# Query norms of half a sequence from four column tiles, inverse roots once per half, in a two-layer transformer kernel on one core

## The chip, the cores and the metric

The kernel runs on one core of one Trainium2 chip, as one launch. The metric is the device time of that launch in microseconds, taken as the median of several runs. Everything is float32, and [...] the profile shows two records (a weight load and a matmul each) for one matmul of the code; a transpose is one record.

The engines are named as in the profile: PE is TensorE's matmuls and PEld its weight loads, DVE is VectorE, ACT is ScalarE, POOL is GpSimd, SP is the engine whose queue issues most of the DMAs. Each engine works through its own queue of instructions in order and waits there for what it needs of the others.

## What is computed

The reference is a model of two layers over 16 sequences of 256 tokens, 128 wide. Each layer is an attention part and a feed-forward part with residuals and layernorms. The change lies in the last of these parts, a causal attention with 16 heads of 64, whose queries and keys are divided by their norm before the scores are made, with a mixture of experts behind it:

```python
def l2norm(x, eps=1e-12):
    return x / jnp.sqrt(jnp.sum(x * x, axis=-1, keepdims=True) + eps)
h = layernorm(x, ln_g, ln_b)
q = (h @ Wq).reshape(B, S, H, DH).transpose(0, 2, 1, 3)
k = (h @ Wk).reshape(B, S, H, DH).transpose(0, 2, 1, 3)
v = (h @ Wv).reshape(B, S, H, DH).transpose(0, 2, 1, 3)
q = l2norm(q) * q_scale
k = l2norm(k) * k_scale
logits = jnp.einsum('bhid,bhjd->bhij', q, k) * QK_SCALE
...
attn = jax.nn.softmax(logits, axis=-1)
out = jnp.einsum('bhij,bhjd->bhid', attn, v)
```

So each token has, for each of 16 heads, a sum of 64 squares of its query and one of its key, and the inverse root of each.

## The kernel before

The 4096 tokens are cut into 8 groups of 512 (two sequences). Each group passes through five stages: A, a dense attention with 16 heads; B, a routed feed-forward; C, a linear and a windowed attention with a gate; D, the causal attention with normed queries and keys; E, the eight experts. Several groups are under way at a time in different stages.

The order of the work is not written by hand. Each piece of work is handed to a planner, `W.add(engine, cost in ns, function, r=reads, w=writes)`, and `Plan.order` (lines 143 to 234) makes a list out of it: again and again it takes the piece that can begin first by its own costs (ties go to the lower `at`, a due time in units of groups), on whichever engine may do it ("VS" means DVE or ACT). The engines then get their instructions in that order. A buffer (`W.buf`) belongs to a class with a fixed number of slots (`SLOTS`, lines 39 to 62: six tiles for `x`, two for `xT`, six for `ud` and so on); a piece can only begin when its buffers have slots, so the number of slots sets how far stages run ahead of each other. `hold` reserves the slot for a later piece. A matmul's `mode` ("f" full, "r" row tiles, "c64" and "c32" column tiles) tells the planner when TensorE changes its tiling. An object such as `chain_d` that several pieces write keeps them in the order in which they were added. The `x` tiles of the first six groups are loaded at the start, those of the last two by the SP queue when a slot is free (`load_x`, line 287).

Stage D (`stage_d`, line 1153) makes a layernorm of the group, transposes it to `hT` (line 1160), and then handles each sequence in two halves of two units; a unit is four heads. There are 64 units in all, 32 halves. `unit` (line 1163) does this:

- the keys of 256 tokens, tokens on partitions (line 1177); ACT squares them into `sq_k` (1178), a copy is kept in `kn` (1179), DVE sums the squares of each head into columns 8 to 15 of `nqk` (1182);
- the queries, already transposed, head by head along the partitions (1191); ACT squares them into `sq_q` (1192), and `keep` (1194) writes them times a scale to `qT`;
- the norms of the queries (1204 to 1207): the squares lie along the partitions, so TensorE adds them up. For each 128 tokens and pair of heads, the 128x128 squares are the stationary operand, and `blk2` (line 487), two columns of ones, one for each head, is the moving one; eight columns come out, tokens on partitions, and DVE copies them to `nqk` (1210);
- `rsqrt` (lines 1135 to 1151): the inverse roots of 16 columns by a bit trick and three Newton steps on DVE, twelve small operations;
- the values (1212), the keys times their inverse roots on POOL (1217), the keys transposed by TensorE (1227) and copied to `kT` (1232);
- two pairs of heads (`pair`, line 568): scores (590), causal mask and maximum on DVE (597, 602, 604), the exponential on ACT with the query's inverse root as scale (623), reciprocal of the sums (630), the weights times it on POOL (636), four or three transposes of the weights (651), and the product with the values (675).

`into_width` (678) then projects the four results of a half.

All matmuls go through `mm` (line 514), where the first argument is the output, then the stationary and the moving operand. The lines of the norms:

```python
for t in range(2):
    for i in range(2):
        mm(pq()[:, 4 * t + 2 * i : 4 * t + 2 * i + 2], sq_q()[:, i * S + t * P : i * S + (t + 1) * P], blk2)
```

Stage C has a place where TensorE works in four column tiles (line 1078): products with `vm` and with `hones` go to 32 output partitions each, four of them side by side.

Of the kernel before, what the change touches and what calls it, by code (L numbers as in the profile page):

```python
# [12 lines left out]
ALU = mybir.AluOpType  # L13
# [17 lines left out]
NFC = FF // P  # L31
NEG = -1.0e30
EPS = 1e-5
NX = 6
NBURST = 2

OFF = {"a": 0.0, "b": 1.0, "c": 2.0, "d": 3.0, "e": 4.0}

SLOTS = (
    ("x", 512, 6),  # L40
    ("xT", 512, 2),
    ("ua", 512, 6),
    ("ud", 512, 6),
    ("pb", 512, 4),
    ("pt", 512, 4),
    ("ov", 256, 8),
    ("m", 64, 26),
    ("k1", 256, 5),
    ("b", 512, 2),
    ("sc", 288, 1),  # L50
    ("c", 512, 9),
    ("qm", 512, 2),
    ("pbC", 512, 2),
    ("ptC", 512, 2),
# [183 lines left out]
def kernel(ctx: ExitStack, tc: tile.TileContext, a: dict, out: bass.AP):  # L238
# [8 lines left out]
    def ctile(name, shape, dtype=F32):  # L247
        return const.tile(shape, dtype, name=name, tag=name)
# [235 lines left out]
        vms.append(ctile(f"vm{i}", [P, 4, D]))  # L484
        nc.gpsimd.memset(vms[i], 0.0)

    blk2 = ctile("blk2", [P, 2])
    nc.gpsimd.memset(blk2, 0.0)
    nc.gpsimd.memset(blk2[:DH, 0:1], 1.0)
    nc.gpsimd.memset(blk2[DH:, 1:2], 1.0)  # L490
    cmask = ctile("cmask", [P, P])
    make_causal_mask(nc, cmask, NEG)
    ones1 = ctile("ones1", [P, 1])
# [2 lines left out]


    chain_a, chain_c, chain_d = ([object() for _ in range(3)] for _ in range(3))
    end_b, end_c = object(), object()

    def pe(n, cols=P, count=1, passes=2):
        return count * passes * max(0.84 * n, 0.87 * cols)
# [62 lines left out]
        else:  # L565
            W.add("V", dve(512), lambda: nc.vector.tensor_scalar(o(), tp(), scale, shift, ALU.mult, ALU.add), r=[tp], w=[o])

    def pair(pi, qT, kT, v, ov, causal, rq):

# [20 lines left out]
        def top():  # L592
            s = sps(S2, a=2)
            n = nmx(n=4, pattern="p (a b) -> p a b", a=2)
            if causal:
                diag = s[:, :, P : 3 * P].rearrange("p a (b k) -> p a b k", k=P)
                nc.vector.tensor_tensor(  # L597
                    out=diag, in0=diag, in1=cmask.unsqueeze(1).unsqueeze(1).to_broadcast([P, 2, 2, P]), op=ALU.add
                )
                for qc in range(2):  # L600
                    c0, nk = col[qc]
                    nc.vector.tensor_reduce(n[:, :, qc], s[:, :, c0 : c0 + nk], AX.X, ALU.max, negate=True)  # L602
                rqp = rq("p (b h) -> p h b", n=8, b=2)[:, 2 * pi : 2 * pi + 2, :]
                nc.vector.tensor_tensor(out=n, in0=n, in1=rqp, op=ALU.mult)  # L604
            else:
                nc.vector.tensor_reduce(n, s.rearrange("p a (b k) -> p a b k", k=S), AX.X, ALU.max, negate=True)  # L606
# [5 lines left out]
        for par in range(2):  # L612
# [3 lines left out]
            def weigh(par=par, pb=pb):  # L616
                s = sps(S2, a=2)
                for qc in range(2):
                    c0, nk = col[qc]
                    kw = {}  # L620
                    if causal:
                        kw["scale"] = rq()[:, qc * 4 + 2 * pi + par : qc * 4 + 2 * pi + par + 1]
                    act(  # L623
                        pb()[:, c0 : c0 + nk], s[:, par, c0 : c0 + nk], AF.Exp,
                        bias=nmx()[:, 2 * par + qc : 2 * par + qc + 1],
                        accum_out=sums()[:, 2 * par + qc : 2 * par + qc + 1], **kw,
                    )
# [507 lines left out]
    def rsqrt(o, x, n, eps):  # L1135

        ve, y, u = W.buf("m", "ve"), W.buf("m", "y"), W.buf("m", "u")

        def go():
            V = nc.vector  # L1140
            V.tensor_scalar(ve(n=n), x(n=n), eps, None, ALU.add)
            yi = y(n=n).bitcast(I32)
            V.tensor_scalar(yi, ve(n=n).bitcast(I32), 1, None, ALU.logical_shift_right)
            V.tensor_scalar(yi, yi, -1.0, float(0x5F3759DF), ALU.mult, ALU.add)
            for k in range(3):
                src, dst = (y, o) if k % 2 == 0 else (o, y)
                V.tensor_mul(u(n=n), src(n=n), src(n=n))  # L1147
                V.scalar_tensor_tensor(u(n=n), u(n=n), -0.5, ve(n=n), ALU.mult, ALU.mult)
                V.scalar_tensor_tensor(dst(n=n), u(n=n), 1.5, src(n=n), ALU.add, ALU.mult)  # L1149

        W.add("V", 2465, go, r=[x], w=[ve, y, u, o])

    def stage_d(g):
        xx = xg[g]
# [5 lines left out]
        transposed(hT, xn, "D", lng2, lnb2)  # L1160
        wqf, wkf = fqk[:, 0, :], fqk[:, 1, :]

        def unit(b, p2):

            W.at = base + (4 * b + p2) / 8
            cs = slice(p2 * 256, (p2 + 1) * 256)
            qT, kT, v = W.buf("ud", "qTD"), W.buf("ud", "kTD"), W.buf("ud", "vD")
            nqk, rqk = W.buf("m", "nqk"), W.buf("m", "rqk")
            ps_q, ps_k, ps_v = W.buf("p", "psq"), W.buf("p", "psk"), W.buf("p", "psv")
            sq_q, sq_k, kn, pq, tps = W.buf("sq", "sqq"), W.buf("sq", "sqk"), W.buf("kn", "kn"), W.buf("p", "pq"), W.buf("p", "tpsk")  # L1170

            def by_tokens(ps, w):
                for t in range(2):
                    mm(ps()[:, t * 256 : (t + 1) * 256], hT()[:, b * S + t * P : b * S + (t + 1) * P], w[:, cs])


            W.add("P", pe(256, count=2), lambda: by_tokens(ps_k, wkf), r=[hT], w=[ps_k], hold=[sq_k, kn])
            W.add("S", scl(512), lambda: act(sq_k(), ps_k(), AF.Square), r=[ps_k], w=[sq_k])
            W.add("VS", (dve(512), scl(512)), lambda e: copy(e, kn(), ps_k()), r=[ps_k], w=[kn])
            W.add(  # L1180
                "V", dve(512),
                lambda: V.tensor_reduce(nqk()[:, 8:16], sq_k("p (h d) -> p h d", d=DH), AX.X, ALU.add), r=[sq_k], w=[(nqk, 1)],
            )


            def proj():
                for i in range(2):
                    p = 2 * p2 + i
                    mm(ps_q()[:, i * S : (i + 1) * S], wqf[:, p * P : (p + 1) * P], hT()[:, b * S : (b + 1) * S])

            W.add("P", pe(S, count=2), proj, r=[hT], w=[ps_q], hold=[sq_q, qT])
            W.add("S", scl(512), lambda: act(sq_q(), ps_q(), AF.Square), r=[ps_q], w=[sq_q])

            def keep(e):
                for i in range(2):
                    c, o = qks[:, 2 * p2 + i : 2 * p2 + i + 1], slice(i * S, (i + 1) * S)
                    if e == "S":
                        A.mul(qT()[:, o], ps_q()[:, o], c)
                    else:
                        V.tensor_scalar(qT()[:, o], ps_q()[:, o], c, None, ALU.mult)  # L1200

            W.add("VS", (782, 714), keep, r=[ps_q], w=[qT])

            def norms():
                for t in range(2):
                    for i in range(2):
                        mm(pq()[:, 4 * t + 2 * i : 4 * t + 2 * i + 2], sq_q()[:, i * S + t * P : i * S + (t + 1) * P], blk2)

            W.add("P", pe(2, count=4), norms, r=[sq_q], w=[pq], hold=[nqk])
            W.add("V", 70, lambda: V.tensor_copy(nqk()[:, 0:8], pq()[:, 0:8]), r=[pq], w=[(nqk, 0)])  # L1210
            rsqrt(rqk, nqk, 16, 1e-12)
            W.add("P", pe(256, count=2), lambda: by_tokens(ps_v, fv), r=[hT], w=[ps_v], hold=[v])
            W.add("SV", (scl(512), dve(512)), lambda e: copy(e, v(), ps_v()), r=[ps_v], w=[v])
            n4 = [P, 8, DH]
            W.add(
                "G", gps(512),
                lambda: G.tensor_tensor(  # L1217
                    out=kn("p (h d) -> p h d", d=DH), in0=kn("p (h d) -> p h d", d=DH),
                    in1=rqk()[:, 8:16].unsqueeze(2).to_broadcast(n4), op=ALU.mult,
                ),  # L1220
                r=[rqk], w=[kn],
            )

            def turn():
                for t in range(2):
                    for i in range(2):
                        nc.tensor.transpose(
                            tps()[:, i * S + t * P : i * S + (t + 1) * P], kn()[:, t * 256 + i * P : t * 256 + (i + 1) * P], ident
                        )

            W.add("P", pe(P, count=4, passes=1), turn, r=[kn], w=[tps], hold=[kT])
            W.add("SV", (scl(512), dve(512)), lambda e: copy(e, kT(), tps()), r=[tps], w=[kT])
            got = []
            for i in range(2):
                W.at = base + (4 * b + p2 + (i + 1) / 3) / 8
                ov = W.buf("ov", "ovD")
                pair(i, qT, kT, v, ov, True, rqk)
                got.append(ov)
            return got

        def seq(b):
            for hf in range(2):
                ovs = unit(b, 2 * hf) + unit(b, 2 * hf + 1)

                def into(ps, hf=hf):
                    o = slice(2 * b * D, (2 * b + 2) * D)
# [36 lines left out]
    def stage_e(g):  # L1283
# [10 lines left out]
        for e_ in range(NE):  # L1294
# [9 lines left out]
            pe_, hids = W.buf("p", "pe"), []  # L1304
            for c in range(NFC):
                ph, hid = W.buf("p", "phE"), W.buf("hid", "hid")
                W.add("P", pe(512), lambda ph=ph, we=we, c=c: mm(ph(), we()[:, c * P : (c + 1) * P], h2()), r=[we, h2], w=[ph], burst=burst, hold=[hid])
                ec = e_ * NFC + c
                W.add("S", 571, lambda ph=ph, hid=hid, ec=ec: act(hid(), ph(), AF.Gelu_apprx_tanh, bias=b1[:, ec : ec + 1]), r=[ph], w=[hid], table="gelut", burst=burst)  # L1309
                hids.append(hid)  # L1310
# [67 lines left out]
```

## Time and profile before

| what | us |
|---|---|
| median of 3 runs | 2264.16 (2259.54 to 2265.47) |
| the profiled execution | 2259.16 |
| its span, first to last instruction | 2257.3 |
| query norms on PE (512 records of 128x2), busy | 62.3 |
| scaling of the keys on POOL (line 1217), 64 times | 67.2 |
| sums of the keys' squares on DVE (line 1182), 64 times | 43.0 |

The granted clock of TensorE was 0.982 of full speed on the mean. In the profile's lists a group is one line of the code on one engine with one kind of operands: the output, an arrow, the inputs, then how many instructions, their busy time together and the mean of one in nanoseconds, and the idle time ahead of them with what ended it. Buffer numbers are left out of the names. In a timeline the columns are the start of a run of like instructions, how long it lasted, engine, line, operation, operands and number. The ends of matmuls are modelled and overlap the next ones; the starts tell more.

### The profile page before, as it was taken

The numbers are of one execution on the slowest core, as the hardware profiler recorded it, in microseconds if no ns is written. First come the engines' busy times: TensorE is split into PE (matmuls) and PEld (weight loads), VectorE is DVE, ScalarE is ACT, GpSimd is POOL, SyncE is SP. The second block draws the span as 40 slices with busy tenths as digits, with TensorE's granted clock in tenths as the row PEclk, the third lists the DMA queues.
The fourth block names the chain that finished last, engine by engine and source line by source line (L and its number), as shares of the span: only waits on it lengthen the run. The fifth ranks groups of instructions, "written<-read, shape, count | busy, mean of one in ns | idle before, by whom it ended". The sixth has DMA issues, their size and how long they took to land.

```text
span 2257.3 us, 50085 instructions
## 1 busy us (share of the span) xinstructions
PE 2126.6 (94%) x18474; PEld 1611.8 (71%) x18474; DVE 1711.4 (76%) x5167; ACT 1316.0 (58%) x3824; POOL 801.7 (36%) x1441
## 2 busy tenths in 40 slices
PE   6999999999999999999999999999899989989987
PEld 5777767777777677776777767777667767767755
DVE  4789898888678977688767897588876976785741
ACT  3556656666466656565565666565565645654642
POOL 6435352444143531335213352143521441330421
PEclk8999999999999999999999999999999999999998
DMA  6100000000100001100010000100011001001101
GB/s 149 24 1 2 2 1 1 2 2 20 43 16 11 2 15 38 34 1 2 15 47 20 2 1 25 48 11 2 1 38 39 7 19 37 22 7 51 29 20 42
DMA packets 61029, 47.98 MB, mean 21 GB/s; under 512 B 4609, under 2 KB 51297, under 8 KB 60785
## 3 DMA queue, kind: packets, MB, share of 16 engines
q1 hardware_dynamic: 59200, 43.09, 6.8%
q8 instruction: 146, 2.39, 0.5%
q0 software_dynamic: 1008, 0.65, 0.3%
q10 hardware_dynamic: 576, 1.05, 0.2%
q14 instruction: 99, 0.80, 0.1%
HBM read 41.89 MB, written 2.88 MB: 20 GB/s over the span
## 4 chain that ended last, share of the span: by engine, by line
PE 31%; DVE 16%; ACT 3%; issue 2%; POOL 1%; POOLq 0%; DVEq 0%; ACTq 0%
PE p L514 25%; PE p L651 2%; PE s L514 2%; DVE m L602 2%; DVE s L597 1%; ACT pb L623 1%; DVE m L606 1%; DVE m L531 1%; POOL pb L636 1%; DVE s L1053 1%; DVE m L1054 1%; PE p L1071 1%; DVE m L1147 1%; DVE pt L522 1%; DVE m L1149 1%
## 5 line engine op out<-in xcount | busy, mean ns | idle before, releaser
L636 POOL TENSOR_SCALAR pb<-pb,m 128x256 f32<-128x256 f32 (+1 forms) x1024 | 452.4, 458 | 710.6 <-DVE m L630 611.2
L1309 ACT ACTIVATE hid<-p,b 128x512 f32<-128x512 f32 x256 | 169.3, 688 | 285.3 <-PE p L514 283.8
L651 PE MATMUL p<-ident,pb 128*128 128x128 f32 x1792 | 293.8, 284 | 22.4 <-POOL pb L636 17.0
L623 ACT ACTIVATE pb<-s,m 128x256 f32<-128x256 f32 x512 | 239.0, 488 | 112.5 <-DVE m L606 100.9
L623 ACT ACTIVATE pb<-s,m,m 128x128 f32<-128x128 f32 (+1 forms) x512 | 257.7, 525 | 62.3 <-DVE m L604 47.7
L651 PEld LDWEIGHTS p<-ident,pb 128*128 128x128 f32 x1792 | 208.1, 143 | 113.6 <-POOL pb L636 66.0
L514 PE MATMUL p<-h,we 128*128 128x512 f32 x512 | 251.5, 624 | 2.9 <-ACT hid L1309 2.5
L514 PEld LDWEIGHTS p<-we,hid 128*128 128x128 f32 x2048 | 238.6, 192 | 15.6 <-issue 10.0
L514 PE MATMUL p<-we,hid 128*128 128x128 f32 x2048 | 246.9, 276 | 1.0 <-ACT hid L1309 0.7
L520 ACT COPY pt<-p 128x384 f32<-128x384 f32 (+1 forms) x316 | 168.9, 541 | 122.6 <-PE p L651 115.7
L1217 POOL TENSOR_TENSOR kn<-kn,m 128x512 f32<-128x512 f32 x64 | 67.2, 1050 | 361.9 <-DVE m L630 224.0
L606 DVE TENSOR_REDUCE m<-s 128x4 f32<-128x1024 f32 x128 | 154.7, 1214 | 32.9 <-PE s L514 32.6
L514 PEld LDWEIGHTS p<-h,we 128*128 128x128 f32 x512 | 93.3, 197 | 98.9 <-issue 63.7
L1324 DVE SCALAR_TENSOR_TENSOR e<-p,m,e 128x128 f32<-128x128 f32 x256 | 71.7, 343 | 111.8 <-PE p L514 89.7
L514 PE MATMUL s<-ua,ua 64*128 64x256 f32 x1024 | 141.9, 401 | 10.9 <-ACT pb L623 10.8
L1065 ACT ACTIVATE pbC<-s,m 128x96 f32<-128x96 f32 (+1 forms) x512 | 135.1, 382 | 16.3 <-DVE m L1054 14.1
L514 PE MATMUL s<-ud,ud 64*128 64x128 f32 (+1 forms) x1024 | 115.7, 347 | 26.1 <-ACT pb L623 25.7
L522 DVE COPY pt<-p 128x512 f32<-128x512 f32 (+1 forms) x196 | 121.1, 623 | 22.1 <-PE p L651 19.9
L514 PE MATMUL p<-pt,ua 128*64 128x256 f32 x1024 | 136.8, 389 | 0.7 <-ACT pt L520 0.7
L602 DVE TENSOR_REDUCE m<-s 128x2 f32<-128x256 f32 (+1 forms) x256 | 130.8, 552 | 4.8
L514 PE MATMUL p<-pt,ud 128*64 128x256 f32 (+1 forms) x1024 | 117.7, 341 | 4.8 <-DVE pt L522 2.6
L514 PEld LDWEIGHTS s<-ua,ua 64*128 64x128 f32 x1024 | 92.0, 189 | 41.7 <-ACT pb L623 19.9
(298 smaller groups left out, 4420.3 us busy)
## 6 DMA issues: line engine op xcount, KB each, us to landing
we<-in_L_ffn_w_dram SPq DMA_DIRECT2D x128, 256.0 KB, 2.7
x<-_attn_hidden_states_dram SPq DMA_DIRECT2D x8, 256.0 KB, 5.3
out_dram<-x SPq DMA_DIRECT2D x8, 256.0 KB, 2.2
dpad<-k SPq DMA_DIRECT2D x1, 768.0 KB, 9.4
wq<-in_L_attn_Wq_dram ACTq DMA_DIRECT2D x2, 256.0 KB
wkv<-in_L_attn_Wkv_dram ACTq DMA_DIRECT2D x2, 256.0 KB, 7.3
wkv<-in_L_attn_Wkv_dram SPq DMA_DIRECT2D x2, 256.0 KB, 7.1
wo<-in_L_attn_Wo_dram SPq DMA_DIRECT2D x1, 512.0 KB, 11.2
```

The lines of the kernel that those rows point to most:

```text
L514: nc.tensor.matmul(o, lhsT=lhsT, rhs=rhs, start=start, stop=stop)
L520: nc.scalar.copy(o, i)
L522: nc.vector.tensor_copy(o, i)
L602: nc.vector.tensor_reduce(n[:, :, qc], s[:, :, c0 : c0 + nk], AX.X, ALU.max, negate=True)
L606: nc.vector.tensor_reduce(n, s.rearrange("p a (b k) -> p a b k", k=S), AX.X, ALU.max, negate=True)
L623: act(pb()[:, c0 : c0 + nk], s[:, par, c0 : c0 + nk], AF.Exp, bias=nmx()[:, 2 * par + qc : 2 * par + qc + 1], accum_out=sums()[:, 2 * par ...
L636: eng.tensor_scalar(pb()[:, c0 : c0 + nk], pb()[:, c0 : c0 + nk], sums()[:, 2 * par + qc : 2 * par + qc + 1], 1.0, ALU.mult, ALU.mult,)
L651: nc.tensor.transpose(tps()[:, at * P : (at + 1) * P], pb()[:, c0 + kc * P : c0 + (kc + 1) * P], ident)
L1065: act(pb("p (u k) -> p u k", u=4)[:, u, :nk], s8[:, hp, :nk], AF.Exp, bias=nmx()[:, hp : hp + 1])
L1217: lambda: G.tensor_tensor(out=kn("p (h d) -> p h d", d=DH), in0=kn("p (h d) -> p h d", d=DH), in1=rqk()[:, 8:16].unsqueeze(2).to_broadcast ...
L1309: W.add("S", 571, lambda ph=ph, hid=hid, ec=ec: act(hid(), ph(), AF.Gelu_apprx_tanh, bias=b1[:, ec : ec + 1]), r=[ph], w=[hid], table="gel ...
L1324: V.scalar_tensor_tensor(m, pe_()[:, j * D : (j + 1) * D], gate()[:, j * NE + e_ : j * NE + e_ + 1], m, ALU.mult, ALU.add)
```

## The change

The query norms are made for half a sequence (two units, eight heads) at once. A new constant `hsum` has, for each of the two units, 32 columns of which two carry ones over the partitions of one head each. It is now the stationary operand, and the squares are the moving one, 128 tokens wide. For each 128 tokens and pair of heads the result goes to 32 partitions of its own, so that four such matmuls stand side by side in four column tiles, and those of the second unit are added to those of the first. The norms then lie with tokens along the free dimension; they are copied to SBUF (`nT`), transposed by TensorE, and gathered into 16 columns of `nqk`. The keys of both units follow, with 16 more columns, and one `rsqrt` of 32 columns serves the half. After it come the values, the scaling, the transposes and the pairs of both units; the projection of the values now also reads `rqk`. `pair` takes its inverse roots from the new places.

The queries of a half stay longer, so they get a class of buffers of their own (`uq`), and other classes lose slots. Up-projections of stage E get a chain, `chain_e`, that keeps them in order.

```diff
-NX = 6
+NX = 5
...
-    ("x", 512, 6),
-    ("xT", 512, 2),
+    ("x", 512, 5),
+    ("xT", 512, 1),
     ("ua", 512, 6),
-    ("ud", 512, 6),
+    ("uq", 512, 3),
+    ("ud", 512, 5),
...
-    ("k1", 256, 5),
+    ("k1", 256, 4),
...
-    ("c", 512, 9),
+    ("c", 512, 8),
...
-    blk2 = ctile("blk2", [P, 2])
...
+    hsum = ctile("hsum", [P, 2, 32])
+    nc.gpsimd.memset(hsum, 0.0)
+    for u in range(2):
+        for h in range(2):
+            nc.gpsimd.memset(hsum[h * DH : (h + 1) * DH, u, 2 * u + h : 2 * u + h + 1], 1.0)
...
-        W.add("V", 2465, go, r=[x], w=[ve, y, u, o])
+        W.add("V", 2465 + 12 * (n - 16), go, r=[x], w=[ve, y, u, o])
...
-                for t in range(2):
-                    for i in range(2):
-                        mm(pq()[:, 4 * t + 2 * i : 4 * t + 2 * i + 2], sq_q()[:, i * S + t * P : i * S + (t + 1) * P], blk2)
-
-            W.add("P", pe(2, count=4), norms, r=[sq_q], w=[pq], hold=[nqk])
-            W.add("V", 70, lambda: V.tensor_copy(nqk()[:, 0:8], pq()[:, 0:8]), r=[pq], w=[(nqk, 0)])
-            rsqrt(rqk, nqk, 16, 1e-12)
...
+                for u in range(2):
+                    for t in range(2):
+                        for i in range(2):
+                            j = 2 * t + i
+                            mm(
+                                pq()[32 * j : 32 * j + 32, :P], hsum[:, u, :], sq_qs[u]()[:, i * S + t * P : i * S + (t + 1) * P],
+                                start=u == 0, stop=u == 1,
+                            )
+
+            W.add("P", 450, norms, r=sq_qs, w=[pq], hold=[nT], mode="c32")
+            W.add("VS", (dve(P), scl(P)), lambda e: copy(e, nT()[:, :P], pq()[:, :P]), r=[pq], w=[nT])
+            W.add("P", 110, lambda: nc.tensor.transpose(pn()[:, :P], nT()[:, :P], ident), r=[nT], w=[pn], hold=[nqk])
             W.add(
-                "V", dve(512),
...
+                "V", 80,
+                lambda: V.tensor_copy(nqk("p (j m) -> p j m", n=16, m=4), pn("p (j m) -> p j m", n=P, m=32)[:, :, :4]),
+                r=[pn], w=[(nqk, 0)],
             )
...
+            rsqrt(rqk, nqk, 32, 1e-12)
+            got = []
+            for u in range(2):
+                W.at = base + (4 * b + 2 * hf + u) / 8
+                kT, v, kn = W.buf("ud", "kTD"), W.buf("ud", "vD"), kns[u]
+                ps_v, tps = W.buf("p", "psv"), W.buf("p", "tpsk")
+                W.add("P", pe(256, count=2), lambda ps_v=ps_v, u=u: by_tokens(ps_v, fv, cols[u]), r=[hT, rqk], w=[ps_v], hold=[v])
...
-                W.add("P", pe(512), lambda ph=ph, we=we, c=c: mm(ph(), we()[:, c * P : (c + 1) * P], h2()), r=[we, h2], w=[ph], burst=burst, hold=[hid])
+                W.add("P", pe(512), lambda ph=ph, we=we, c=c: mm(ph(), we()[:, c * P : (c + 1) * P], h2()), r=[we, h2], w=[ph, chain_e], burst=burst, hold=[hid])
```

## The prediction

> **What bounds the kernel now.** I read the page's head first, then busy time in stretches of 100 us, then the list of waits of TensorE alone.
>
> ```profile
> span 2257.3 us, 50085 instructions
> PE 2126.6 (94%) x18474; PEld 1611.8 (71%) x18474; DVE 1711.4 (76%) x5167; ACT 1316.0 (58%) x3824; POOL 801.7 (36%) x1441
> ...
> 0.00:100.00 100.00, 81.77 (x524) 61.25 (x524) 54.90 (x119) 42.25 (x145) 53.74 (x120) 0.93 0.43 97
> ...
> 300.00:400.00 100.00, 90.03 (x817) 70.65 (x817) 87.31 (x293) 68.27 (x203) 42.70 (x74) 0.98 0.01 2
> 400.00:500.00 100.00, 98.91 (x1065) 78.26 (x1064) 85.73 (x233) 65.91 (x224) 40.59 (x79) 0.99 0.01 2
> ...
> 2100.00:2200.00 100.00, 88.49 (x585) 63.15 (x585) 60.99 (x211) 51.35 (x150) 31.06 (x61) 0.95 0.08 22
> ...
> PE s L514 <- ACT pb L623: 37.0, 29, 5.3
> PE p L651 <- POOL pb L636: 17.0, 9, 10.2
> ```
>
> PE is busy in 94% of the span; in the stretches (columns: length, then busy us of PE, PEld, DVE, ACT, POOL) it is 88 to 99 us of each hundred once the first is over. What PE lacks, 2257.3 - 2126.6 = 131 us, is 18 us of start-up, some 28 us after 2100 where only the last group is left, and small waits, the largest kind 37 us in all. So a microsecond of work taken off PE is a microsecond of time, unless it comes back as a wait. DVE at 76% is the next engine, and 86 to 91% in some stretches. A busy PE is not an exact measure, since matmuls overlap: work is priced below by the distance from one group's start to the next.
>
> **What goes.** Per unit (64 of them) PE makes the norms with eight records of 128x2, each with a 128x128 weight load:
>
> ```profile
> 708.37 0.49 PE L651 MATMUL p<-ident,pb 128*128 128x128 f32 x3
> 708.79 0.65 PE L514 MATMUL p<-ptC,vm 96*32 96x64 f32 x32
> 709.26 0.63 PE L514 MATMUL p<-ptC,hones 96*32 96x64 f32 x32
> 709.82 0.87 PE L514 MATMUL p<-pt,ud 128*64 128x256 f32 x8
> ...
> 718.56 0.95 PE L514 MATMUL p<-blk,sq 128*128 128x2 f32 x8
> 719.37 0.53 PE L651 MATMUL p<-ident,pb 128*128 128x128 f32 x3
> ...
> 726.06 0.95 PE L514 MATMUL p<-blk,sq 128*128 128x2 f32 x8
> 726.94 1.08 PE L514 MATMUL p<-pt,ua 128*64 128x256 f32 x8
> ```
>
> 719.37 - 718.56 = 0.81 us, 726.94 - 726.06 = 0.88 us; the middle, 0.85, times 64 is **54.4 us off PE** (51.8 to 56.3).
>
> On DVE, half of the 64 root sequences go. Twelve operations of 128x16 each: the three lines of the Newton steps are 37.8 + 36.6 + 37.0 us, the three before them 12.4 + 15.0 + 14.3, 153.1 us in all; the 64 small copies of line 1210 are 64 x 0.156 = 10.0 us.
>
> **What comes, on PE.** Per half (32 of them) 16 records with 32 weight columns and 128 moving columns in four column tiles. The nearest row is the window sums above, `hones`: 32 records of 64 columns in four column tiles, the same number of columns. Its sister `vm`, followed by the same mode, takes 709.26 - 708.79 = 0.47 us; `hones`, followed by another mode, 0.56, so leaving a mode costs 0.09. Entering costs the same: three transposes take 0.42 us before `vm` where 3 x 0.11 = 0.33 is usual. A half costs 0.47 + 0.09 + 0.09 = 0.65 us, 32 halves **20.8 us**; the far end, tiles that don't overlap, is rival D. The built program agrees: 844 changes between kinds of tiling against 779, 65 more. One 128x128 transpose per half at 0.11 us (a run of transposes steps by 0.11): **3.5 us**. Work on PE: -54.4 + 20.8 + 3.5 = **-30.1 us**.
>
> [...] The row: 0.47 us for 32 records is 14.7 ns each. [...]
>
> **What comes, on DVE and ACT.** 32 root sequences of 12 operations on 128x32, priced by lines 799 and 813 of that shape (220 and 241 ns): 12 x 0.22 = 2.64 us, 84.5 us. 32 gathering copies of 128x16 at about 0.16, 5 us. 32 copies of 128x128 from PSUM, 18 on DVE and 14 on ACT in the built program, at 0.309 (copies of up to 129 columns): 5.6 and 4.3 us. DVE: -163.1 + 84.5 + 5 + 5.6 = **-68 us** of 1711. That is off the bound. It counts only through PE waits that a busy DVE causes: outside start-up and the last 57 us there are 131 - 18 - 16 = 97 us of idle PE; 4% less DVE work, 4% of them, **-4 us** (bounds: 0, and half of the 34 us that PE idles in 100:500, 700:800, 1000:1100 and 1500:1600, where DVE is over 85%, -17).
>
> **New waits.** Two, both on PE, which runs in order, so that all later matmuls queue behind them and ACT and DVE behind those.
> The transpose waits for the copy of the norms. In the built order 0.9 to 4.2 us of other PE work stand between (median 1.5, by the rows' spacings); it needs a copy of 0.31 and two hand-overs of about 0.15. Nearest row: line 855's transposes, also of a tile just made, idled 2.6 + 0.9 us (DVE, ACT) at 8 places, 0.44 each. Ends 0 and 32 x 0.44 = 14; with the work between I take 0.1 each, **+3 us**.
> The first turn of keys in a half waits for the roots, now of both units:
>
> ```profile
> 325.54 0.67 DVE L1182 TENSOR_REDUCE m<-sq 128x8 f32<-128x512 f32 x1
> ...
> 328.36 0.17 DVE L1141 TENSOR_SCALAR m<-m 128x16 f32<-128x16 f32 x1
> ...
> 330.66 0.17 DVE L1149 SCALAR_TENSOR_TENSOR m<-m,m 128x16 f32<-128x16 f32 x1
> 331.01 1.04 POOL L1217 TENSOR_TENSOR kn<-kn,m 128x512 f32<-128x512 f32 x1 [5.54 <-DVE m L1149]
> 332.11 0.42 PEld L1227 LDWEIGHTS p<-ident,kn 128*128 128x128 f32 x4
> ```
>
> The roots run 328.36 to 330.83, POOL follows after 0.18, PE 0.06 after POOL. From the last key projection: square 0.60, sum 0.67, roots 2.6, POOL 1.05, hand-overs 0.6: 5.5 us. In the built order 4.6 to 17.6 us of PE work stand there (median 8.2); two places are under 5.5, eight under 6.8. Half a microsecond at eight places: **+4 us**. Below, nothing is to be won: the old trace has 0.6 us of PE waits for `kn` on PE's own list; above stands rival C.
>
> **Edits at nothing.** The fewer slots: one `x` less delays the load of group 5 until group 0 is stored, but the built order has 106 us of PE work between group 0's last expert and that group's first transpose (101 in the old one for its group 6), against 5.3 us for a load; if that cover went, PE would stand for the tail of the norm, store and load, some 10 us at three places. One `xT`, `ud`, `c` and `k1` less change what the planner interleaves; counted in PE work, the new order ends each group's attention in stage D 7 to 41 us sooner than the old, so nothing in it has been pushed back. `chain_e` only fixes an order on PE itself: no wait. The value projections move behind the roots, where they fill PE's wait. Six fewer table loads (65 to 59) on ACT, 1.28 us each, lie beside PE. Copies of `qT` and squares are as many as before.
>
> **Sum.** -30.1 - 4 + 3 + 4 = -27 us. The profiled execution took 2259.2 us (span 2257.3 and 1.9 around it): 2232. The median of the three runs is 5 us above it, so for a median I say **2235 us**.
>
> **Rivals.** (A) The forecast, 2220 to 2250: 60%. (B) The freed DVE pays more and no wait appears: -30.1 - 17, 2212: 12%. For it, DVE near 90% in those stretches; against, PE is at 98.9 in 400:500 with DVE at 86. (C) Slower: the first turn of a half becomes the stall. If two softmax jobs of the causal pairs stand on DVE ahead of the roots (lines 597, 602 twice, 604: 0.69 + 2 x 0.55 + 0.23 = 2.0 us each), the chain is 9.5 us; summed over the 32 places what the order's distances lack of it is about 48 us: 2259 - 30 + 48 = 2277. It decides from 30 us, 0.94 per half. For it, distances were planned, not measured, and both units now hang on one root; against, those 0.6 us in the old trace, whose chain was as long. 15%. (D) The column tiles don't overlap, as if the change had no tiles: 16 x 0.107 = 1.71 us a half instead of 0.47, +40, 2272: 5%; the window sums speak against it. [...]
>
> **Numbers.** Range 2210 to 2262: it leaves out most of C, D and the lower edge of B, under 2 in 10. A change within 0.3% (7 us) can't be told from none. Faster: A, B, most of E and a little of C, 0.80; same 0.08; slower, C and D for the most part, 0.12.
>
> **What would show it.** Right: PE's busy time near 2095 us, a `sq,hsum` group stepping to its successor in 0.5 to 0.6 us, DVE near 1640, 32 root sequences at 2.5 to 2.7 us. Wrong: PE's idle time over 150 us with waits of `ident,kn` for POOL (C) or of the new transpose for a copy; [...] waits of `ident,x` for a DMA, if the `x` slot was needed.

## The result, and the profile after

The changed kernel takes 2235.34 us in the median (2233.45 to 2238.21), the kernel before on the same chip 2261.85 (2259.29 to 2265.47): ratio 0.9877, 95% interval 0.9859 to 0.9894, 26.5 us less. The forecast was 2235. That the sum came out does not mean that its terms did; two of them were wrong, and it was luck that they nearly made up for each other.

The head of the page of the changed kernel: the span, then busy time, share and number of instructions of each engine.

```profile
span 2236.3 us, 49748 instructions
...
PE 2103.2 (94%) x18506; PEld 1566.6 (70%) x18506; DVE 1662.7 (74%) x4784; ACT 1308.2 (58%) x3817; POOL 799.6 (36%) x1443
```

PE lost 23.4 us of busy time (2126.6 before), and its idle time rose from 130.7 to 133.1 (span less busy). Of the predicted 30 us of PE work, 23 are there.

The groups of PE that bear on it, from the list of groups of the changed kernel (operands, number, then busy us and mean ns, then the idle time ahead and what ended it):

```profile
L516 PE MATMUL p<-h,we 128*128 128x512 f32 x512 | 265.5, 619 | 9.5 <-ACT hid L1339 4.9 <-DVE e L1354 2.6 <-DVE ud L524 0.8
L516 PE MATMUL p<-sq,hsum 128*32 128x128 f32 x512 | 20.5, 278 | 0.2 <-DVE uq L1201 0.2
L1219 PE MATMUL p<-ident,k 128*128 128x128 f32 x32 | 9.5, 295 | 1.2 <-DVE k L524 1.2
```

and the first of them in the kernel before:

```profile
L514 PE MATMUL p<-h,we 128*128 128x512 f32 x512 | 251.5, 624 | 2.9 <-ACT hid L1309 2.5 <-DVE m L1274 0.3
```

The norms went from 62.3 us of busy records to 20.5, and the new transpose waits 1.2 us in all. The up-projections of the experts, of which not one was added, show 14 us more of busy time and wait for 6.6 us more. They are what `chain_e` orders. Most of the 14 us is a matter of counting: a record that stands last before other work counts with its whole modelled end. From each start to the next, less idle time, the up-projections take 238.7 us in the kernel before and 239.7 in the changed one.

One half's norms in the timeline of PE of the changed kernel (start, length, line, operands, number):

```profile
326.97 0.64 PE L516 MATMUL p<-sq,hsum 128*32 128x128 f32 x16
327.55 0.66 PE L655 MATMUL p<-ident,pb 128*128 128x128 f32 x4
328.04 1.95 PE L516 MATMUL p<-wo,ov 128*128 128x128 f32 x16
329.82 0.27 PE L1219 MATMUL p<-ident,k 128*128 128x128 f32 x1
329.93 1.25 PE L516 MATMUL p<-fqk,d 128*128 128x256 f32 x5
```

The sixteen records step by 0.58 us to the next group (0.57 in the median of the 32 halves), the transpose by 0.11.

The root sequence on DVE, from the groups of the changed kernel:

```profile
L1152 DVE SCALAR_TENSOR_TENSOR m<-m,m 128x32 f32<-128x32 f32 x96 | 21.6, 225 | 3.3
L1153 DVE SCALAR_TENSOR_TENSOR m<-m,m 128x32 f32<-128x32 f32 x96 | 20.9, 218 | 3.3
L1151 DVE TENSOR_TENSOR m<-m 128x32 f32<-128x32 f32 x96 | 20.4, 212 | 3.3
...
L1148 DVE TENSOR_SCALAR m<-m 128x32 int32<-128x32 int32 x32 | 7.1, 222 | 1.1
L1147 DVE TENSOR_SCALAR m<-m 128x32 int32<-128x32 int32 x32 | 6.7, 209 | 1.2
L1145 DVE TENSOR_SCALAR m<-m 128x32 f32<-128x32 f32 x32 | 5.5, 171 | 0.3
```

Together 82.2 us, 2.57 per sequence. What PE waited for, in the changed kernel (us in total, times, longest):

```profile
PE s L516 <- ACT pb L627: 30.3, 27, 4.3
PE p L655 <- POOL pb L640: 13.9, 10, 9.3
PE p L516 <- ACT hid L1339: 6.9, 11, 0.9
PE p L1258 <- POOL kn L1248: 6.9, 11, 1.2
```

and of the same list in the kernel before, the two that grew:

```profile
PE p L514 <- ACT hid L1309: 3.1, 7, 1.1
...
PE p L1227 <- POOL kn L1217: 0.6, 1, 0.6
```

The wait for scaled keys (`kn`) rose from 0.6 us to 6.9, that for `hid` from 3.1 to 6.9; the two kinds of softmax wait (`pb`) fell by 10 together, from 37.0 and 17.0. A wait on PE holds up what stands behind it: in the trace of the kernel before, PE's 18474 records start in the order of the built program, two for each of its 7848 matmuls and one for each of its 2778 transposes, but for 22 among the column tiles of stage C; on DVE the same holds for all 5167.

### The profile page after: what moved, and what is told of

The parts are those of the page before. It is cut to its first block, busy times and chain, and to the rows that moved or that the text cites. A ratio compares the mean times of both kernels' runs of the same rounds, so it can differ in the third digit from the quotient of the medians.

```text
span 2236.3 us, 49748 instructions
## 1 busy us (share of the span) xinstructions
PE 2103.2 (94%) x18506; PEld 1566.6 (70%) x18506; DVE 1662.7 (74%) x4784; ACT 1308.2 (58%) x3817; POOL 799.6 (36%) x1443
## 4 chain that ended last, share of the span: by engine, by line
PE 54%; DVE 19%; ACT 5%; issue 2%; POOL 2%; POOLq 0%; DVEq 0%; ACTq 0%
PE p L516 39%; PE s L516 7%; PE p L655 5%; DVE m L605 2%; ACT pb L627 2%; PE p L1075 2%; DVE s L600 1%; DVE m L533 1%; DVE m L609 1%; DVE x L546 1%; POOL pb L640 1%; DVE m L607 1%; PE p L1258 1%; DVE e L1354 1%; DVE uq L1201 1%
## 5 line engine op out<-in xcount | busy, mean ns | idle before, releaser
L655 PE MATMUL p<-ident,pb 128*128 128x128 f32 x1792 | 291.3, 283 | 23.4 <-POOL pb L640 13.9
L627 ACT ACTIVATE pb<-s,m 128x256 f32<-128x256 f32 x512 | 238.7, 489 | 70.1 <-DVE m L609 59.7
L516 PE MATMUL p<-h,we 128*128 128x512 f32 x512 | 265.5, 619 | 9.5 <-ACT hid L1339 4.9
L516 PEld LDWEIGHTS p<-we,hid 128*128 128x128 f32 x2048 | 241.1, 193 | 29.4 <-issue 15.7
L522 ACT COPY pt<-p 128x512 f32<-128x512 f32 (+1 forms) x316 | 168.6, 540 | 144.2 <-PE p L655 132.3
L609 DVE TENSOR_REDUCE m<-s 128x4 f32<-128x1024 f32 x128 | 154.4, 1214 | 27.1 <-PE s L516 26.1
L516 PE MATMUL s<-ud,uq 64*128 64x128 f32 (+1 forms) x1024 | 118.9, 355 | 21.3 <-ACT pb L627 20.3
L516 PEld LDWEIGHTS p<-h,we 128*128 128x128 f32 x512 | 85.6, 194 | 64.8 <-issue 31.1
L1024 POOL TENSOR_TENSOR qm<-c,hm 128x512 f32<-128x512 f32 x64 | 68.1, 1069 | 153.9 <-PE s L516 134.2
```

What stands on the lines that cost most here:

```text
L516: nc.tensor.matmul(o, lhsT=lhsT, rhs=rhs, start=start, stop=stop)
L522: nc.scalar.copy(o, i)
L627: act(pb()[:, c0 : c0 + nk], s[:, par, c0 : c0 + nk], AF.Exp, bias=nmx()[:, 2 * par + qc : 2 * par + qc + 1], accum_out=sums()[:, 2 * par ...
L655: nc.tensor.transpose(tps()[:, at * P : (at + 1) * P], pb()[:, c0 + kc * P : c0 + (kc + 1) * P], ident)
L1024: (V if e == "V" else G).tensor_tensor(out=qm("p (h q) -> p h q", q=QC), in0=qw()[:, c0 : c0 + QC].unsqueeze(1).to_broadcast(nq), in1=hm8. ...
```

## The experiments

Each kernel was timed beside the kernel before, whose median was between 2261.85 and 2264.56 from one comparison to the next; so a difference between medians, as given below, is sure to some 3 us. The ratio to the kernel before stands with its interval.

**The norms, first try.** Old norms in the new structure, the order planned anew:

```diff
-mm(pq()[32 * j : 32 * j + 32, :P], hsum[:, u, :], sq_qs[u]()[...], start=u == 0, stop=u == 1)
+c = 4 * (2 * t + i) + 2 * u
+mm(pq()[:, c : c + 2], sq_qs[u]()[...], blk2)
-W.add("P", 450, norms, ..., mode="c32")
+W.add("P", pe(2, count=8), norms, ...)
```

> The changed kernel with its halves and its one root sequence per half, but the query norms made as before: 256 matmuls of two columns with the squares as weights, no column tiles, no extra transpose. Theory PE: the gain is the price of the norms on PE. 64 x 0.85 = 54 us come back and 32 x (0.57 + 0.11) = 22 us go, so about 2235 + 32 = 2267 us, no faster than before the change. Rival DVE: the gain comes from the 32 root sequences that were saved; they stay saved here, so 2235 to 2245 us.

Measured: 2330.18, ratio 1.0288 (1.0274 to 1.0302), 95 us above the changed kernel and far from every figure expected. The same without `chain_e`:

> Halves and one root sequence per half, query norms as before the change (squares as weights, two moving columns), and no chain in stage E: it differs from the kernel without chain (2216 us) in the form of the norms alone. Theory PE: the norms cost 64 x 0.86 instead of 32 x 0.66 us, so 2216 + 34 = 2250 us, and what the kernel with old norms and chain lost beyond that (2330 us) was the chain's. Rival: old norms fit badly into halves whatever stage E does: above 2290.

Measured: 2314.67, ratio 1.023 (1.0216 to 1.0243), 98 above its partner, the next kernel. Neither is a price of the norms alone: the planner had made another order around blocks of 1.7 us, and the table at the end of this section splits the 98 into three parts, of which only the 36 us of PE work lie near the 34 expected. The pair says that `chain_e` costs about the same with either norms (15.5 here), and that the price of the norms had to be taken in an order that stays.

**The chain of up-projections away.**

```diff
-    w=[ph, chain_e], burst=burst, hold=[hid])
+    w=[ph], burst=burst, hold=[hid])
```

> The changed kernel without the chain that orders the up-projections of stage E. Theory: the chain splits the up-projections into single matmuls between other work (163 runs of two records in the changed kernel's trace, 26 before), and the busy time of that group rose by 14 us, the term that the prediction lacked; without the chain the runs join again and the time falls by 5 to 12 us, to 2223 to 2230. Rival: the splitting comes from the new order as a whole, not from the chain: 2230 to 2240 with as many single runs.

Measured: 2216.41 (2214.84 to 2219.91), ratio 0.9789 (0.9776 to 0.9803): **18.9 us faster than the change as made**, more than the 5 to 12 expected. Its head and its up-projections:

```profile
span 2213.4 us, 49851 instructions
...
PE 2092.0 (95%) x18506; PEld 1565.4 (71%) x18506; DVE 1662.1 (75%) x4793; ACT 1312.3 (59%) x3818; POOL 798.0 (36%) x1443
```

```profile
L516 PE MATMUL p<-h,we 128*128 128x512 f32 x512 | 245.9, 612 | 6.3 <-ACT hid L1339 4.1 <-DVE pt L524 1.6 <-DVE m L1304 0.5
```

Against the changed kernel PE is busy 11.2 us less and idle 11.7 less (121.4), in profiled executions that lie 22.9 us apart. What the chain does to the order shows in PE's timeline of the changed kernel:

```profile
812.38 1.02 PE L516 MATMUL p<-c,wkw 128*128 128x512 f32 x2
813.24 1.02 PE L516 MATMUL p<-h,we 128*128 128x512 f32 x2
814.10 1.03 PE L516 MATMUL p<-wlkv,c 128*128 128x256 f32 x4
814.96 1.02 PE L516 MATMUL p<-h,we 128*128 128x512 f32 x2
815.82 1.03 PE L516 MATMUL p<-wlkv,c 128*128 128x256 f32 x4
816.68 1.02 PE L516 MATMUL p<-h,we 128*128 128x512 f32 x2
```

and without the chain at the same place:

```profile
811.98 2.74 PE L516 MATMUL p<-h,we 128*128 128x512 f32 x6
814.56 1.89 PE L516 MATMUL p<-wlkv,c 128*128 128x256 f32 x8
```

An up-projection is one matmul, two records. Chained, they stand one at a time with other work between: 154 such lone pairs in the changed kernel, 30 without the chain, 24 in the kernel before (the expectation's 163 and 26 also count runs that only a pause cuts). The code says why: in the planner a piece that depends on one on its own engine may begin 80 ns after it (`OWN`, lines 89 and 173), so that a chained projection is never the first that can begin, and any other ready piece goes between. A lone pair steps no more than usual (814.10 - 813.24 = 0.86, and 2 x 0.431 in the median), so splitting as such is not the price; the price is in the order that comes of it. About half of it is waits. Which of these waits follow from which split is open.

**The new norms twice, same order.** The loop of sixteen records runs two times over.

> The changed kernel with each group of norms issued twice (the second time over the first), the planner's costs and so the order as they were. Theory PE: 16 records more per half at 0.47 us, 32 x 0.47 = 15 us, 2250 us. [...] If a record of another tile did not overlap: 32 x 1.7 = 55 us, 2290. If PE were not the bound: 2235.

Measured: 2252.9, ratio 0.9946 (0.9933 to 0.9958): +17.5 by the medians, 0.55 us for sixteen records (+15.6 by the ratios, 0.49; by the steps in the trace 0.44, or 14 us). In its timeline the doubled group steps by 1.02 us:

```profile
326.40 1.08 PE L516 MATMUL p<-sq,hsum 128*32 128x128 f32 x32
327.42 0.66 PE L655 MATMUL p<-ident,pb 128*128 128x128 f32 x4
```

1.02 less 0.58 is 0.44 us for the second sixteen, 28 ns a record. The trace also shows how they lie: in all 32 halves of the changed kernel the sixteen records start in four bursts of four, each burst within 0.05 us and 0.11 to 0.14 us after the one before. A record of 128 columns steps by 0.11 us where tiles are not used (the sixteen of `wo,ov` above: 1.78 us), so four records go here in the time of one there.

**The order of the tiles.** The loops over tiles outside, over units inside, so that two records in a row go to the same tile.

> The changed kernel with the eight norm matmuls of a half in another order: both units of one column tile one after the other, then the next tile, so that neighbours meet in the same tile more often; same work and same planned order. Theory column tiles: records of one tile don't overlap, a half takes up to 4 x 4 x 0.107 = 1.7 us instead of 0.57, at most +36 us, and about half of that since the last record of a tile overlaps the first of the next: 2250 to 2270. Rival: the records are short because of the narrow weight load or the issue, not because the tiles work side by side: 2235, no change.

Measured: 2236.89, ratio 0.9887 (0.9875 to 0.99), no difference to the changed kernel; a group steps by 0.59 us:

```profile
326.96 0.66 PE L516 MATMUL p<-sq,hsum 128*32 128x128 f32 x16
327.55 0.66 PE L655 MATMUL p<-ident,pb 128*128 128x128 f32 x4
```

The expected rise did not come; the time is the rival's. Yet in 31 of the 32 halves the records start in four bursts of four here too, 0.11 us apart: they do not follow one another singly, as short ones would, but start four at a time. In the program neighbouring matmuls did not have to go to different tiles for it (0.59 us a group here, 0.58 there). The trace does not say which tile each record of a burst went to, so why the order makes no difference is open.

**The old norms in an order that stays.** First in the kernel without the chain, as an addition to the new ones:

```diff
+for u in range(2):
+    for t in range(2):
+        for i in range(2):
+            c = 256 + 4 * (2 * t + i) + 2 * u
+            mm(pq()[:, c : c + 2], sq_qs[u]()[...], blk2)
```

> The changed kernel without chain_e (2216 us), with the old norms issued as well, right behind the new ones and into columns of the same PSUM tile that nothing reads; the order of all other work is the same. The prediction priced these records at 64 x 0.85 = 54.4 us. If that is their price, 2271 (2265 to 2277). If the 98 us by which the planned kernel with the old norms lies above the one with the new (2315 against 2216) are the price of the records themselves, by the clock that they cost PE, 2295 or more. If the records lie beside waits of PE, under 2260.

Measured: 2283.82, ratio 1.0078 (1.0063 to 1.0092): +67.4, between the two figures. Then in the kernel before, its own norms doubled:

> The kernel before (2262 us) with its norms computed twice, the second time into the same columns; the order is the same. By the price of the prediction (0.85 per unit, 64 units) 2316 (2310 to 2322); if the time answers to PE work in front of the norms' waits more than one for one, 2335 or more; if it lies in slack, under 2300.

Measured: 2315.88, ratio 1.0223 (1.0208 to 1.0238): +52.0 to the kernel before of the same runs, 0.81 per unit. As a net price the 54.4 of the prediction stands here. It is not the price of the records alone: in the table below, PE's work rises by 44 us and the clock's part by 29, while 14 us of idle time are filled.

**The roots twice, same order.** The twelve operations of each root sequence run two times over, with the same result; DVE has 71 us more of work.

> The changed kernel with the twelve operations of each root sequence done twice, the order as it was. It gives DVE back 32 x 2.5 = 80 us and the chain in front of the first keys of a half 2.5 us. Theory PE: little of it shows, by the 4% rule of the prediction +5 us, with the longer chain up to +15: 2240 to 2250. Rival DVE: the whole gain goes and more, 2260 or above.

Measured: 2333.78, ratio 1.0304 (1.029 to 1.0318): **+98 us**, more than the added work itself. PE's list of waits in this kernel begins:

```profile
PE p L1259 <- POOL kn L1249: 50.4, 25, 3.8
PE s L516 <- ACT pb L627: 29.1, 26, 4.4
PE p L655 <- POOL pb L640: 23.7, 15, 10.7
```

The wait for the scaled keys goes from 6.9 to 50.4 us: this is where rival C put it. The edit does two things at once, it loads DVE and it makes the chain ahead of the first keys some 2.2 us longer, and the list of waits points to the second. With the planner told of it (the sequence's cost doubled too, chain kept):

> The changed kernel with every root sequence done twice as in the run that took 2334 us, but with the doubled cost told to the planner, which may put other work in front of the first keys. Theory: the 98 us were a chain that the plan had left no room for; with room they fall to 5 to 25 us, 2240 to 2260. Rival: DVE itself carries the time, 2300 or above with the plan too.

Measured: 2282.14, ratio 1.009 (1.0077 to 1.0103): +47, with 15.7 us of that wait. Both expectations missed: the time lies between them. So half of the 98 us was a plan that left no room, and the other half is the cost that remains when the plan knows (DVE's busy time is 55 us up in it, some copies having moved to ACT). That half is not DVE's load alone, since the order is another one and the longer chain is still there.

**The roots shared less.** Without the chain, two sequences a half again, of 24 and 8 columns; the second unit's keys have their own.

> No chain, new norms, but two root sequences per half: one of 24 columns (the queries of both units and the keys of the first), one of 8 (the keys of the second). It undoes the sharing of the roots alone. DVE gets 32 x 12 x 0.18 = 69 us back, planned for. Theory PE: DVE is beside the bound, 2216 to 2230. Rival DVE: the saved root sequences carry the gain, about 2216 + 25 to 60. A gain below 2210 would say that the wait of the first unit for the second's keys costs more than the roots.

Measured: 2261.98, ratio 0.9998 (0.999 to 1.0007): +46 to the kernel without the chain, and all its gain is gone. DVE has 43 us more work, and PE 12 more of busy and 35 more of idle time. The waits are not where the roots are:

```profile
PE s L516 <- ACT pb L627: 34.0, 37, 4.1
PE p L655 <- POOL pb L640: 19.3, 9, 11.7
PE p L516 <- ACT hid L1341: 10.7, 17, 1.1
PE p L516 <- ACT pt L522: 10.2, 9, 2.5
PE p L1260 <- POOL kn L1250: 7.1, 9, 1.4
```

The same five kinds come to 31.2, 12.8, 5.0, 4.3 and 1.9 without the split, 26 us less. Softmax, its copies and the experts wait a little more each; with the roots doubled and planned the first three kinds also rose, to 41.7, 18.1 and 14.5 us from the 30.3, 13.9 and 6.9 of the changed kernel. Two cautions. The edit also makes another plan, in which ACT is 24 us busier, so the 46 us are not DVE's alone. And this kernel has as many root sequences as the kernel before, DVE as busy (1705.3 us, 1711.4 before), the cheap norms and no chain, but it is no faster than the kernel before: PE is idle for 156.8 us, where it was 130.7. So the step to halves by itself seems to cost waits, which the shared roots win back; 46 us is what the sharing is worth in this structure, not against the kernel before.

**The slots.** The kernel before with as few slots of `x`, `xT`, `k1` and `c` as the changed one:

> The kernel before with the numbers of slots of x, xT, k1 and c that the changed kernel has (5, 1, 4, 8 instead of 6, 2, 5, 9), planned anew. The prediction cost these at nothing: 2255 to 2269. If the fewer slots are what the step to halves pays (the changed structure with the old norms and no chain_e took 2315), 2285 or more.

Measured: 2260.44, ratio 0.998 (0.9973 to 0.9988), with 2263.85 for the kernel before in the same comparison. And the kernel without the chain with the slots of `k1` and `c` given back:

> The changed kernel without chain_e, with one more slot of k1 and of c, as many as before, planned anew (x and xT stay at 5 and 1). If slots cost nothing, 2216 again (2209 to 2223); if the planner lacks room for the two loops that use these tiles, 2205 or less, and then it is the fastest of all; over 2223 if another order by itself moves the time by some 10 us.

Measured: 2217.78, ratio 0.9793 (0.978 to 0.9806). Slots move the time by 3.4 and 1.4 us, though both kernels are planned anew; that is also how little another order need matter by itself.

Not tried: the new norms alone in the kernel before, unit by unit, and `chain_e` alone in it. For both the planner came to a point where no piece of work could begin.

**The profiled executions in three parts.** The last section shows that TensorE's granted clock is at times 0.50. In the changed kernel's trace a transpose then steps by 0.214 us in the median instead of 0.109, an up-projection by 0.853 a record instead of 0.431. So half of PE's busy time at that clock is what the clock cost, the rest of its busy time is work, and what is left of the span is idle time. This is an estimate from the traces, one execution each; more waits also add a little "work", since a record before a wait counts with its whole modelled end.

| kernel | PE work | clock | idle | span, us |
|---|---|---|---|---|
| before | 2100.5 | 26.1 | 130.7 | 2257.3 |
| before, norms doubled | 2144.6 | 54.9 | 116.8 | 2316.4 |
| changed | 2075.7 | 27.5 | 133.1 | 2236.3 |
| changed, roots doubled | 2079.8 | 58.7 | 195.9 | 2334.4 |
| the same, planned | 2081.8 | 35.7 | 162.9 | 2280.4 |
| no chain | 2069.1 | 22.9 | 121.4 | 2213.4 |
| no chain, roots split | 2073.1 | 30.9 | 156.8 | 2260.8 |
| no chain, old norms added | 2121.9 | 43.5 | 117.9 | 2283.3 |
| no chain, old norms instead, new plan | 2105.0 | 62.0 | 145.8 | 2312.8 |

The last row lies 99 us above "no chain": 36 of work, 39 of clock and 24 of waits. The chain's 22.9 us are 6.6, 4.6 and 11.7.

## Why the prediction was right, and where not

The sum, by what the runs show, in medians: old norms -52, new ones +17.5, their transposes +3.5 (32 x 0.11, from the trace), `chain_e` +19: -12. The measured change is -26.5, so all the rest of the half structure, the shared roots and their waits, gave -14.5. This last number is a difference of several and was not measured by itself: with the 67 that the old norms cost in the other kernel it would be about zero. The table supports it in another way. From the kernel before to the one without chain PE's work fell by 31.4 us, where the record had 30.1, the clock's part by 3.2 and the idle time by 9.3, so the rest gave some 12.5. The record had -54.4 + 20.8 + 3.5, nothing for the chain, and +3 for the rest. Two errors, 19 and some 15 to 17 us, of opposite sign.

- **What bounds the kernel now.** Half right. Matmuls put in lengthen the time by about their length or more (52 and 67 for 54, 16 to 17.5 for 14), so PE is the bound. But work that PE never does moves the time as much: 71 us on DVE, put in front of the keys, cost 98, or 47 when planned for. At 94% busy, the missing 6% still answers to DVE.
- **What goes.** Right on PE. The root sequences went as computed.
- **What comes, on PE.** Right, a little dear: 0.57 us a half where 0.65 was put, since the second sixteen show that entering and leaving the tiling cost 0.58 - 0.44 = 0.14 together, not 0.18. Rival D (1.71 us) falls with it. PE's busy time is 2103, not 2095; the chain's 11 us of busy time are more than that difference.
- **What comes, on DVE and ACT.** The work was sized well: 82.2 us of roots where 84.5 was put. DVE's busy time fell by 49, not 68; by the sums of the rows, which count overlaps twice, it fell by 62, since copies there rose by 10. **The term that failed is the worth of it**, "4% less DVE work, 4% of them, -4 us": the share of PE's idle time is no measure, because it counts only waits that exist now, and each wait has a chain behind it. The split roots, at 43 us of DVE work for 46 us of time, and the 47 for the doubled roots when planned, say that it was far more than 4, though both hold another plan and the halves' own waits. Against the kernel before, the sum leaves -14.5 with the new waits in it, and -22 if their 7.5 us are taken out: at or past the -17 that stood as the outer bound.
- **New waits.** Right in place and size: 1.2 us at the transpose where 3 was put, 6.3 more for `kn` where 4 was put. The doubled roots show how near rival C was: the wait it named came there, 50.4 us of it, and the plan had left just enough room.
- **Edits at nothing.** Right for the slots of the four classes that were tried (those of `ud` and `uq` were not). **Wrong for `chain_e`, "only fixes an order on PE itself: no wait".** It is a rule for the planner, and the planner answered by laying up-projections apart; 18.9 us. The order of PE's records alone shows it: 154 lone pairs against 24.
- **Rivals.** B came nearest in what the rest was worth and was wrong in the time, since it knew nothing of the chain either; without the chain the time is 2216, near its 2212. Its "no wait appears" was wrong: `kn` waits 6.3 us more.

The best kernel here is the change without `chain_e`, 2216.41 us, 2.1% under the kernel before.

## What to carry to other kernels

An edit that only names an order has a price like any other: count in the built program how many runs of like work it breaks up before it is put at nothing. The worth of freed time on an engine that is not the bound cannot be read from the share of busy time; double the suspected work in an unchanged order, and again with the plan told of it, and the first number less the second says how much was room in the plan. The price of a group of instructions is to be taken in an order that stays, and split into work, clock and waits: by new plans the old norms seemed to cost 98 us, in a fixed order they cost 52 and 67.

## What the runs showed of the clock

In the changed kernel's trace the 26 records of TensorE's granted clock hold it at 1.00 or 0.50, each for 3.41 us or a whole multiple of it (the last one is cut by the end). Stretches of that length in the changed kernel (columns: length, then busy us of PE, PEld, DVE, ACT and POOL with their instructions, PE's clock, DMA share, GB/s):

```profile
801.21:804.62 3.41, 1.59 (x4) 0.58 (x5) 2.17 (x4) 2.84 (x4) 0.00 (x0) 1.00 0.00 0
804.62:808.03 3.41, 3.41 (x5) 1.35 (x5) 0.00 (x0) 1.60 (x3) 0.00 (x0) 0.50 0.20 49
808.03:811.44 3.41, 3.41 (x27) 2.93 (x26) 0.75 (x1) 0.69 (x1) 2.45 (x3) 1.00 0.09 33
```

PE is idle for 1.82 us of the first stretch, and the next runs at half clock. Counted over the changed kernel and the seven others with the new norms only, after the first 25 us: of 91 full-clock stretches with at least 1.7 us of idle PE, in one piece or several, 82 were followed by one at half clock; of 227 with 0.9 to 1.7 us, 16; of some 4200 with less than 0.3 us, none. In the changed kernel alone it was 10 of 10, 2 of 25 and none of 528. By what rule the clock falls, these counts do not say. But in these runs an idle PE is paid for again: with the roots doubled, the idle time grew by 63 us (133.1 to 195.9), the mean clock fell from 0.982 to 0.968, and the clock's part in the table grew by 31 us, together 94 of the 98.

Beside records with two moving columns the clock also fell after stretches with little idle time; the runs do not agree on it. In the kernel before with doubled norms:

```profile
324.88:328.30 3.42, 3.21 (x24) 2.97 (x23) 3.42 (x8) 0.51 (x1) 1.00 (x2) 1.00 0.00 0
328.30:331.71 3.41, 3.41 (x20) 2.93 (x18) 3.00 (x17) 1.17 (x2) 0.23 (x1) 0.50 0.02 5
```

The first stretch holds only 0.2 us of idle PE, but sixteen records of `blk,sq` from 325.47 on. In this kernel and the one with old norms added, 81 full-clock stretches have less than 0.3 us of idle PE but at least 1.2 us of idle and norm records together: 18 of them were followed by half clock, and none of the 1022 with less. In the two kernels with the old norms instead of the new, which have the same blocks of sixteen, there are 52 such stretches, and one was followed by half clock. So two moving columns are not enough by themselves; what else it takes is open.

The clock's part rose by 29 us with the norms of the kernel before doubled, and by 21 with the old norms added. In the second this is enough to explain why 54 became 67; in the first, PE's idle time fell by 14 us and hid part of it.
